# A planned AdaLN block on one core: smaller last pieces, split statistics and another list of leads

## The chip, the core and the metric

The kernel runs on one core of a Trainium2 chip, whose other cores do nothing. Five engines take part, each with an instruction queue of its own that runs in order: TensorE (PE in the profile; PEld is its weight load), VectorE (DVE), ScalarE (ACT), GpSimd (POOL) and SyncE (SP), which here only issues DMA transfers. The metric is the device time of one execution in microseconds (us), from several runs of which the median is taken.

## The reference

The input `x` holds 8 batches of 1024 tokens with 128 features, in float32. Six modulation vectors come from a conditioning vector `c`, and two sub-blocks are added onto `x`:

```python
mod = (_silu(L0_c) @ L0_wmod).reshape(B, 6, 1, -1)
sa, ca, ga, sb, cb, gb = (mod[:, 0], ..., mod[:, 5])
ga = (2 * (ga >= 0) - 1) * jnp.maximum(jnp.abs(ga), 0.25)      # gb likewise
h = _layernorm(x, axis=-1) * (1 + ca) + sa
x = x + ga * attn(h)
h = _layernorm(x, axis=-1) * (1 + cb) + sb
x = x + gb * ffn(h)
```

`attn` is six layers of linear attention, each followed by a multilayer perceptron:

```python
for i in range(6):
    xn = _layernorm(x, ln1_w[i], ln1_b[i])
    q, k, v = heads(xn @ wq[i]), heads(xn @ wk[i]), heads(xn @ wv[i])   # 8 heads of 16
    context = einsum('bhnd,bhne->bhde', softmax(k, over tokens), v)
    x = merge(einsum('bhnd,bhde->bhne', softmax(q, over features), context)) @ wo[i] + bo[i] + x
    hdn = leaky_relu(_layernorm(x, ln2_w[i], ln2_b[i]) @ w1[i], 0.01)   # 128 -> 512
    x = hdn @ w2[i] + x                                                 # 512 -> 128
```

`ffn` has 352 hidden features and rounds both operands of each product to a four-bit float grid, with one scale for every 16 values (`fp4_quant_dequant`):

```python
gate, y = fp4_linear(x, w_gate), fp4_linear(x, w_up)
return fp4_linear(silu(gate) * y, w_down)
```

## The kernel before

A batch lies in SBUF as 128 partitions by 8 chunks (`C`) of 128 features, token = partition x 8 + chunk. It is worked on in two halves (`H`) of 4 chunks (`HC`), 512 columns each, which is one PSUM bank. Four lanes (`LANES`) hold the buffers of four batches, so up to four batches are under way; batch b+4 takes the buffers of batch b.

Each batch passes eight stages: stage 0 is the first modulated layernorm, stages 1 to 6 are the six layers, stage 7 is the FFN and the store. `layernorm` (L571) makes per chunk one `bn_stats` (L587) and one `bn_aggr` (L589) on VectorE, then for the half a logarithm and an exponential on ScalarE (L603, L608), four small VectorE steps that refine the reciprocal root and make the shift (L613 to L629), and last the scaled rows, half on VectorE (L635) and half on ScalarE (L642). The eight statistics instructions of a half are one step, `moments`. `transposed` (L655) turns a half with TensorE (L661). A layer then has its products on TensorE (keys L892, queries L939, the context L1002 to L1036, the output L1069, the perceptron L1115 and L1132), its softmaxes on VectorE and ScalarE with the query scaling on POOL (L980), and its additions onto `x` on VectorE (L1054).

`ffn` (L1145) takes the modulated norm of both halves, rounds each half (`fp4`, L668), and turns it. For every chunk there are two products of 352 columns (L1176), the silu on ScalarE (L1184) and the gate's product on VectorE (L1192). The gated values lie in four groups (`NQ`) of G = 2 chunks, 704 columns. Each group is rounded by `fp4`: on VectorE a maximum per 16 values (L689), the scale (L696), its reciprocal (L701) and a product (L705); on ScalarE the magnitude (L715); on VectorE two steps that round (L719, L726); on POOL the product with the scale (L733). Then TensorE turns the group (L1207), ScalarE copies it out of PSUM (L1222), TensorE multiplies it by `w_down` with the modulation folded in (L1233) and VectorE adds it onto `x` (L1242). After the second and fourth group a half of 256 KB is stored (L1250). The buffers of `fp4` and the turned group `gT` exist twice, and groups alternate between the two sets.

Nothing is issued while this code runs. Every piece of work is a step handed to a planner (`Plan`), with its engine, its estimated time (`occ`), what it reads and writes, and a priority. `Plan.order` (L143) then simulates the engines and puts the steps in one order. At each turn it takes, over all engines, the step that can start first by its estimate; among those that start together, the one with the longest chain of work behind it (`tail`) plus its lead. The lead comes from the table `LEAD[batch][stage]`; `TURNS` changes entries of it at given times of the simulation, as (time, [(batch, stage, lead), ...]). Steps without a stage, such as the preparation of weights and of the later modulation (`aside`), have the lead -`LATE`, in part with more taken off. Steps with `port=True` on VectorE and all on POOL are kept apart by the simulation, so that the two do not use the port to SBUF that they share at one time. Eight PSUM banks are handed out by the simulation too.

The planner also keeps TensorE's clock up. Where TensorE would stand still for more than `GAP` (0.6 us), it puts in dummy products of the identity with itself (`warm`, L1287) into a free bank, and stops `BRINK` short of the next real step. Before the time `COLD` it takes a dummy product for twice as long. The resulting order is fixed by dependencies between neighbours on each engine's queue.

Of the kernel before, what the change touches and what calls it, by code (L numbers as in the profile page):

```python
# [14 lines left out]
P = 128  # L15
# [47 lines left out]
class Ps:  # L63


    n = 0
# [17 lines left out]
class Plan:  # L84
# [5 lines left out]
    GAP, BRINK, COLD = 0.6, 0.15, 6.0  # L90
# [52 lines left out]
    def order(self, leads, turns, warm):  # L143
# [17 lines left out]
        while todo:  # L161
# [22 lines left out]
            gap = e == "PE" and t - free[e] > self.GAP  # L184
            while gap and min(bank_free) <= free[e]:
                to = free[e] + (2 if free[e] < self.COLD else 1) * mm(P)
                if to > t - self.BRINK:
                    break
                w, bank = Step(), bank_free.index(min(bank_free))
                w.fn, w.func = lambda bank=bank: warm(bank), None  # L190
                free[e] = bank_free[bank] = to
                out.append(w)
# [3 lines left out]
            end = now + s.occ  # L196
# [38 lines left out]
def mm(n):  # L235

    return 0.01 + n * 1.66e-3
# [11 lines left out]
def kernel(  # L249
# [41 lines left out]
        [2428, 4186, 594, 344, -1166, -1149, -1333, -3656],  # L291
        [-878, 557, 2162, 224, -3438, -84, 492, -1524],
        [1136, -253, -1456, -2344, -3625, 1683, -2362, -2313],
# [8 lines left out]
        (75, [(1, 1, 582)]),  # L302
        (90, [(3, 1, 625)]),
        (135, [(2, 2, -1493)]),
        (315, [(2, 2, -332)]),
        (330, [(2, 2, -1493)]),
        (435, [(1, 4, -3891)]),
        (450, [(1, 4, -3438)]),
        (480, [(2, 4, -5886)]),
        (495, [(2, 4, -3663)]),  # L310
        (675, [(2, 7, -1993), (4, 2, -2394), (4, 3, -1963)]),
        (840, [(4, 4, -73)]),
        (1050, [(5, 6, -1896)]),
        (1095, [(4, 6, -2129)]),
        (1125, [(4, 6, -55), (5, 7, -1056)]),
        (1185, [(4, 7, -1051)]),
        (1215, [(6, 6, -416), (6, 7, -409)]),
        (1230, [(7, 5, -1069)]),
        (1245, [(4, 7, -1061)]),
        (1275, [(7, 5, -1070), (7, 6, -414)]),  # L320
        (1350, [(7, 6, -432)]),
        (1365, [(6, 7, -1605), (7, 7, -1614)]),
    ]
    LATE = 70.0
    NQ = 4
    FCOLS = C // NQ * I

# [243 lines left out]
    def layernorm(ln, dst, src, h, n, HV=HC // 2):  # L571


        stats = Buf(lanes_p, [P, HC, 6], f"stats{h}{ln}", f"stats_{n}{h}")
# [9 lines left out]

        def moments():
            for c in range(HC):
                nc.vector.bn_stats(stats.ap()[:, c, :], s(c))  # L587
# [3 lines left out]
        add("DVE", HC * 0.264, moments, r=at(src, h), w=[stats, mv])  # L591
# [76 lines left out]
    def fp4(src, parts, ncol, n, i):  # L668
# [13 lines left out]
        def each(t):  # L682
# [47 lines left out]
        )  # L730
        add(
            "POOL", pool2(ncol),
            lambda: nc.gpsimd.tensor_tensor(  # L733
                blocks(src()), blocks(vv()), each(s()), ALU.mult
            ),
            r=[v, scale], w=parts,
# [408 lines left out]
    def ffn(x, mod, b, ln):  # L1145
# [49 lines left out]
        for i, g in enumerate(gs):  # L1195
            fp4(lambda g=g: g.ap()[:, : G * I], g.parts, G * I, f"g{b}_{i}", i % 2)

            gT = Buf(work, [P, NK * G * P], f"gT{i % 2}", f"gT_{b}_{i}", 2)
            whole = I // P
            tts = [Ps(psum), Ps(psum)]  # L1200

            def turn(g, tt, m0, m1):
                for m in range(m0, m1):
                    k, kk = KS[m]
                    for c in range(G):
                        o = ((m - m0) * G + c) * P
                        nc.tensor.transpose(  # L1207
                            tt.ap()[:kk, o : o + P],
                            g.ap()[:, c * I + k : c * I + k + kk], ident,
                        )  # L1210

            for part, (m0, m1) in enumerate(((0, whole), (whole, NK))):
                kk = KS[m1 - 1][1]
                n = (m1 - m0) * G * P
                add(
                    "PE", (m1 - m0) * G * TRANSPOSE,
                    lambda g=g, tt=tts[part], m0=m0, m1=m1: turn(g, tt, m0, m1),
                    r=[g], w=[tts[part]],
                )
                add(  # L1220
                    "ACT", act(n),
                    lambda gT=gT, tt=tts[part], m0=m0, kk=kk, n=n: nc.scalar.copy(  # L1222
                        gT.ap()[:kk, m0 * G * P : m0 * G * P + n], tt.ap()[:kk, :n]
                    ),
                    r=[tts[part]], w=[gT[part]],
                )
            td = Ps(psum)

            def dmm(gT=gT, td=td):
                for c in range(G):  # L1230
                    for m, (k, kk) in enumerate(KS):
                        o = (m * G + c) * P
                        nc.tensor.matmul(  # L1233
                            td.ap()[:, c * D : (c + 1) * D], gT.ap()[:kk, o : o + P],
                            wdb.ap()[:kk, m, :], start=(m == 0), stop=(m == NK - 1),
                        )

            add("PE", G * NK * mm(D), dmm, r=[gT, wdb], w=[td])

            def onto(i=i, td=td):  # L1240
                xc = x.ap()[:, i * G * D : (i + 1) * G * D]
# [107 lines left out]
```

## Time and profile before

| what | before |
|---|---|
| median of 3 runs | 1419.99 us (1418.98 to 1420.02) |
| profiled execution: its time | 1418.91 us |
| profiled execution: its span, first to last instruction | 1417.3 us |
| granted clock of TensorE over the span | 0.999 |
| TensorE busy | 1400.6 us, of it 33.5 in tile `warm` |
| VectorE busy | 1148.7 us |
| ScalarE busy | 987.7 us |
| POOL busy | 249.7 us |
| last store issued, and landed after | 1414.1 us, 2.0 us |

A row of a group or of a timeline gives the engine, the line of the kernel, the operation, what it writes and reads by the program's tile names, the shapes and the count. In a timeline the two numbers in front are the start and the time covered in us; what stands in brackets is how long the engine stood idle before it and whose work ended that. A float32 product appears as two MATMUL records, a float32 turn as one. Matmuls overlap in their pipeline, so a record's duration (275 ns for 128 columns) is longer than the distance from one to the next (0.11 us). VectorE's records overlap a little in the same way.

### The profile page before, as it was taken

How to read it: one execution, taken by the hardware profiler on the slowest of the kernel's cores; microseconds unless marked ns; L12 is line 12 of the kernel's file. 1: busy time of each engine (PE TensorE's matmuls, PEld its weight loads, DVE VectorE, ACT ScalarE, POOL GpSimd, SP SyncE). 2: the span in 40 equal slices, each digit the busy share in tenths (PEclk: the TensorE clock that was granted, in tenths of full speed). 3: DMA queues.
4: the chain of work that ended last, by engine and by line, in shares of the span. 5: the costliest groups of instructions: out<-in, count | busy, mean ns of one | idle time of the engine just before them, and what ended most of it. 6: DMA issues, size and time to landing. Idle time of an engine off the chain costs nothing. (4 is left out here: it accounts for less than half of the span.)

```text
span 1417.3 us, 26401 instructions
## 1 busy us (share of the span) xinstructions
PE 1400.6 (99%) x9257; PEld 1124.6 (79%) x9257; DVE 1148.7 (81%) x4491; ACT 987.7 (70%) x2286; POOL 249.7 (18%) x215
## 2 busy tenths in 40 slices
PE   9999999999999999999999999999999999999998
PEld 7787788787787788778877887778778887787787
DVE  8996768776688887798989886587897767999986
ACT  6885856766667767676766675676776667867763
POOL 2220101010112112122231110011223111112222
PEclk9999999999999999999999999999999999999999
DMA  7100000000000000000000000000000000000000
GB/s 224 39 1 1 2 1 1 1 2 1 1 16 12 1 16 1 15 12 16 17 26 1 16 1 1 1 1 1 12 16 1 1 1 1 1 1 5 5 23 31
DMA packets 16004, 18.78 MB, mean 13 GB/s; under 512 B 1552, under 2 KB 9848, under 8 KB 15872
## 3 DMA queue, kind: packets, MB, share of 16 engines
q1 hardware_dynamic: 15872, 17.10, 3.8%
q8 instruction: 73, 1.20, 0.4%
q14 instruction: 59, 0.48, 0.1%
HBM read 12.88 MB, written 4.22 MB: 12 GB/s over the span
## 5 line engine op out<-in xcount | busy, mean ns | idle before, releaser
L1115 PE MATMUL ps<-xT_m,w_sb 128*128 128x512 f32 x768 | 349.7, 593 | 1.5 <-DVE g L1192 1.2
L1115 PEld LDWEIGHTS ps<-xT_m,w_sb 128*128 128x128 f32 x768 | 137.2, 190 | 132.0 <-issue 92.5
L980 POOL TENSOR_TENSOR q<-q,qsum 128x512 f32<-128x512 f32 x96 | 102.2, 1073 | 629.5 <-DVE qsum L975 195.2
L1054 DVE TENSOR_TENSOR x<-ps,x 128x512 f32<-128x512 f32 x192 | 129.9, 681 | 101.4 <-PE ps L1132 83.3
L603 ACT ACTIVATE rstd_a<-mv_a,eps 128x4 f32<-128x4 f32 x96 | 28.6, 298 | 125.3 <-DVE mv_a L589 105.2
L939 PEld LDWEIGHTS ps<-wq_sb,xT_a 128*128 128x128 f32 x768 | 95.5, 192 | 24.3 <-issue 16.3
L642 ACT ACTIVATE xh_a<-x,shift_a,rstd_a 128x128 f32<-128x128 f32 x192 | 84.0, 489 | 38.0 <-DVE shift_a L629 36.8
L1132 PEld LDWEIGHTS ps<-w_sb,hT_D 128*128 128x128 f32 x640 | 86.8, 192 | 15.0 <-issue 11.7
L939 PE MATMUL ps<-wq_sb,xT_a 128*128 128x128 f32 x768 | 98.2, 275 | 0.5 <-ACT g L1184 0.5
L1132 PE MATMUL ps<-w_sb,hT_E 128*128 128x128 f32 x640 | 97.6, 275 | 0.0
L1132 PE MATMUL ps<-w_sb,hT_C 128*128 128x128 f32 x640 | 97.6, 275 | 0.0
L1132 PE MATMUL ps<-w_sb,hT_B 128*128 128x128 f32 x640 | 97.6, 275 | 0.0
L1132 PE MATMUL ps<-w_sb,hT_D 128*128 128x128 f32 x640 | 97.5, 275 | 0.0
L1069 PEld LDWEIGHTS ps<-m,qT 128*128 128x128 f32 x768 | 91.1, 192 | 7.3 <-issue 2.8
L892 PE MATMUL ps<-xT_a,wk_sb 128*128 128x512 f32 x192 | 95.4, 595 | 1.0 <-ACT xT_a L872 0.6
L1069 PE MATMUL ps<-m,qT 128*128 128x128 f32 x768 | 95.2, 276 | 0.8 <-DVE m L1043 0.8
L1002 PEld LDWEIGHTS ps<-k,xh_a 128*128 128x128 f32 x768 | 90.5, 192 | 6.5 <-issue 3.8
L1002 PE MATMUL ps<-k,xh_a 128*128 128x128 f32 x768 | 93.4, 275 | 0.2 <-DVE x L1054 0.2
L642 ACT ACTIVATE xh_m<-x,shift_m,rstd_m 128x128 f32<-128x128 f32 x192 | 82.6, 489 | 10.5 <-DVE shift_m L629 9.9
L872 ACT ACTIVATE xT_a<-ps,cols 128x512 f32<-128x512 f32 x96 | 72.1, 775 | 19.2 <-PE ps L661 18.8
L587 DVE BATCH_NORM_STATS2 stats_a<-x 128x6 f32<-128x128 f32 x384 | 82.9, 278 | 2.9 <-POOL x L855 0.9
L1132 PEld LDWEIGHTS ps<-w_sb,hT_B 128*128 128x128 f32 x640 | 84.4, 192 | 0.5 <-ACT xh_m L642 0.2
(180 smaller groups left out, 3263.8 us busy)
## 6 DMA issues: line engine op xcount, KB each, us to landing
x<-in_L_attn_x_dram SPq DMA_DIRECT2D x16, 256.0 KB, 3.3
out_dram<-x SPq DMA_DIRECT2D x16, 256.0 KB, 2.0
w_sb<-in_L_attn_w_dram SPq DMA_DIRECT2D x12, 256.0 KB, 4.3
mod<-mod_d SPq DMA_DIRECT2D x8, 256.0 KB, 3.7
mod<-mod_d SPq DMA_DIRECT2D x4, 128.0 KB, 3.6
wmod_b<-in_L_wmod_dram SPq DMA_DIRECT2D x1, 384.0 KB, 3.6
wk_sb<-in_L_attn_wk_dram SPq DMA_DIRECT2D x6, 64.0 KB, 3.5
wq_sb<-in_L_attn_wq_dram SPq DMA_DIRECT2D x6, 64.0 KB, 3.5
```

The lines of the kernel that those rows point to most:

```text
L587: nc.vector.bn_stats(stats.ap()[:, c, :], s(c))
L603: lambda: nc.scalar.activation(y(), var(), AF.Ln, bias=eps),
L642: nc.scalar.activation(d(c), s(c), AF.Identity, bias=shift.ap()[:, c : c + 1], scale=rstd.ap()[:, c : c + 1],)
L872: lambda t=t, h=h: nc.scalar.activation(half(xT, h), t.ap(), AF.Identity, bias=col(params + 1, l), scale=col(params, l),),
L892: lambda tk=tk, h=h: nc.tensor.matmul(tk.ap(), wk_sb[:, l, :], half(xT, h), start=True, stop=True),
L939: nc.tensor.matmul(tq.ap()[:, c * D : (c + 1) * D], half(xT, h)[:, c * P : (c + 1) * P], wq_sb[:, l, :], start=True, stop=True,)
L980: lambda h=h, hs=hs: nc.gpsimd.tensor_tensor(heads(half(q, h)), heads(half(q, h)), each(qsum.ap()[:, hs]), ALU.mult),
L1002: nc.tensor.matmul(tc_.ap()[:, :D], chunks(xh.ap())[:, c, :], chunks(k.ap())[:, c, :], start=(c == 0), stop=(c == C - 1),)
L1054: lambda: nc.vector.tensor_tensor(half(x, h), t.ap(), half(x, h), ALU.add),
L1069: nc.tensor.matmul(to.ap()[:, c * D : (c + 1) * D], half(qT, h)[:, c * P : (c + 1) * P], m.ap(), start=True, stop=True,)
L1115: lambda th=th, h=h, j=j: nc.tensor.matmul(th.ap(), w1_sb[:, l, j * P : (j + 1) * P], half(xmT, h), start=True, stop=True,),
L1132: nc.tensor.matmul(ty.ap()[:, c * D : (c + 1) * D], hidden(j)[:, c * P : (c + 1) * P], w2g.ap()[:, j, :] if l == L - 1 else w2_sb[:, l, j, :],
```

## The change

Four things are changed together.

- The last batch's FFN ends in smaller pieces. The work behind the gates is moved into a function `down`, which is called for every entry of `PIECES`: for batches 0 to 6 four groups of two chunks, as before; for batch 7 two groups of two chunks and then four of one chunk. Of the last piece alone `fp4` does the final product with the scale on VectorE instead of POOL. Batch 7 is stored in four parts of 128 KB, each after its two chunks, instead of two of 256 KB. The pieces still alternate between two sets of buffers.
- The statistics of a half are no longer one step. Each of its four `bn_stats` is a step of its own, which depends on the part of the source that it reads, and the four `bn_aggr` are one more step. The planner may place other VectorE work between them.
- In the planner `COLD` is 7.5 instead of 6.0. Before that time a real TensorE step takes twice its estimate in the simulation, and a gap is filled with dummy products from half of `GAP` on.
- The leads are others: a few entries of `LEAD`, the whole list `TURNS` (57 times instead of 21), and `LATE` is 140 instead of 70.

What is computed stays the same.

```diff
-    GAP, BRINK, COLD = 0.6, 0.15, 6.0
+    GAP, BRINK, COLD = 0.6, 0.15, 7.5
...
-            gap = e == "PE" and t - free[e] > self.GAP
+            cold = 2 if e == "PE" and free[e] < self.COLD else 1
+            gap = e == "PE" and t - free[e] > self.GAP / cold
             while gap and min(bank_free) <= free[e]:
-                to = free[e] + (2 if free[e] < self.COLD else 1) * mm(P)
+                to = free[e] + cold * mm(P)
...
-            end = now + s.occ
+            end = now + s.occ * (2 if e == "PE" and now < self.COLD else 1)
...
     LEAD = [
-        [2428, 4186, 594, 344, -1166, -1149, -1333, -3656],
-        [-878, 557, 2162, 224, -3438, -84, 492, -1524],
-        [1136, -253, -1456, -2344, -3625, 1683, -2362, -2313],
+        [2420, 4178, 586, 336, -1174, -1157, -1341, -3664],
+        [158, 557, 2162, 224, -3448, -84, 492, -1524],
+        [1202, -253, -1456, -2344, -3625, 1683, -2362, -2313],
...
     TURNS = [
-        (75, [(1, 1, 582)]),
-        (90, [(3, 1, 625)]),
...
-        (1350, [(7, 6, -432)]),
-        (1365, [(6, 7, -1605), (7, 7, -1614)]),
+        (15, [(2, 1, -124)]),
+        (45, [(0, 2, 1600), (3, 0, -324)]),
...
+        (1305, [(6, 7, -440), (7, 6, -443)]),
+        (1320, [(7, 6, 40)]),
+        (1335, [(4, 7, -2064), (5, 7, -2271), (6, 7, -2282), (7, 6, 278), (7, 7, 207)]),
     ]
-    LATE = 70.0
+    LATE = 140.0
...
+    PIECES = (
+        [(i, i * C // NQ, C // NQ) for i in range(NQ)],
+        [(0, 0, 2), (1, 2, 2), (0, 4, 1), (1, 5, 1), (0, 6, 1), (1, 7, 1)],
+    )
+    DVE_LAST = True
...
+        for c in range(HC):
+            add(
+                "DVE", 0.197, lambda c=c: nc.vector.bn_stats(stats.ap()[:, c, :], s(c)),
+                r=at(src, h)[c * H // HC :][:1], w=[stats[c]],
+            )
+
         def moments():
             for c in range(HC):
-                nc.vector.bn_stats(stats.ap()[:, c, :], s(c))
-            for c in range(HC):
                 nc.vector.bn_aggr(mv.ap()[:, c, :], stats.ap()[:, c, :])

-        add("DVE", HC * 0.264, moments, r=at(src, h), w=[stats, mv])
+        add("DVE", HC * 0.067, moments, r=[stats], w=[mv])
...
-    def fp4(src, parts, ncol, n, i):
+    def fp4(src, parts, ncol, n, i, last="POOL"):
...
-        add(
-            "POOL", pool2(ncol),
-            lambda: nc.gpsimd.tensor_tensor(
-                blocks(src()), blocks(vv()), each(s()), ALU.mult
-            ),
-            r=[v, scale], w=parts,
+        eng = nc.vector if last == "DVE" else nc.gpsimd
+        add(
+            last, (vec if last == "DVE" else pool2)(ncol),
+            lambda: eng.tensor_tensor(blocks(src()), blocks(vv()), each(s()), ALU.mult),
+            r=[v, scale], w=parts, port=True,
         )
...
+        for i, c0, cn in PIECES[b == B - 1]:
+            down(gs[c0 // G], c0 % G, cn, c0, wdb, x, f"{b}_{c0}", i % 2, DVE_LAST and b == B - 1 and c0 + cn == C)
+            done = c0 + cn
+            if b == B - 1 and done % G == 0:
+                parts, n = [x[done // G - 1]], G
+            elif b < B - 1 and done % HC == 0:
+                parts, n = at(x, done // HC - 1), HC
+            else:
+                continue
+            add(
+                "SP", move(64 * n),
+                lambda done=done, n=n: nc.sync.dma_start(
+                    out[:, done - n : done, :], chunks(x.ap())[:, done - n : done, :]
+                ),
+                r=parts,
+            )
+
+    def down(g, g0, G, c0, wdb, x, name, i, last):
+        def src():
+            return g.ap()[:, g0 * I : (g0 + G) * I]
+
+        parts = g.parts[g0 : g0 + G]
+        fp4(src, parts, G * I, f"g{name}", i, "DVE" if last else "POOL")
+
+        gT = Buf(work, [P, NK * C // NQ * P], f"gT{i}", f"gT_{name}", 2)
...
+        add("PE", G * NK * mm(D), dmm, r=[gT, wdb], w=[td])
...
+        add("DVE", vec(G * D), onto, r=[td], w=[x[c0 // (C // NQ)]])
```

## The prediction

> **What bounds the kernel now.** First I read the page's busy times and its slices.
>
> ```profile
> PE 1400.6 (99%) x9257; PEld 1124.6 (79%) x9257; DVE 1148.7 (81%) x4491; ACT 987.7 (70%) x2286; POOL 249.7 (18%) x215
> ...
> PE   9999999999999999999999999999999999999998
> ...
> PEclk9999999999999999999999999999999999999999
> ```
>
> TensorE (PE) is busy for 99% at the full granted clock, so only the matmul time itself seems to be left. But part of that busy time is filler: the planner puts dummy matmuls (tile `warm`) into TensorE's gaps. So the second view is busy time by stretches, first of everything, then (after its own heading line) of tile `warm` alone.
>
> ```profile
> 0.00:100.00 100.00, 95.11 (x641) 77.77 (x642) 91.65 (x451) 75.71 (x200) 26.79 (x32) 1.00 0.31 94
> 100.00:600.00 500.00, 499.56 (x3324) 400.85 (x3323) 378.99 (x1563) 345.11 (x809) 61.34 (x56) 1.00 0.02 5
> 600.00:1372.00 772.00, 764.87 (x4997) 609.77 (x4997) 646.76 (x2411) 546.91 (x1238) 149.94 (x120) 1.00 0.02 7
> 1372.00:1418.00 46.00, 41.10 (x302) 36.15 (x300) 31.26 (x68) 20.02 (x43) 11.62 (x8) 0.97 0.08 30
> ...
> core 0: us, PE busy (x) PEld busy (x), PEclk, DMA share, GB/s
> 0.00:100.00 100.00, 17.35 (x124) 15.91 (x124) 1.00 0.31 94
> 100.00:600.00 500.00, 0.00 (x0) 0.00 (x0) 1.00 0.02 5
> 600.00:1372.00 772.00, 4.47 (x30) 3.81 (x30) 1.00 0.02 7
> 1372.00:1418.00 46.00, 11.70 (x96) 11.27 (x96) 0.97 0.08 30
> ```
>
> Columns: PE, PEld, DVE, ACT, POOL busy, clock, DMA. Idle plus filler on TensorE is the loss: 4.9 + 17.4 = 22.2 us in the first 100; 0.4 in the next 500; 7.1 + 4.5 = 11.6 from 600 to 1372; and 4.9 (4.2 without the 0.7 behind the span) + 11.7 = 15.9 at the end. Together 50 us. The change removes no matmul, so it can work on these 50 us alone.
>
> Last, the timeline of the end.
>
> ```profile
> 1396.32 2.39 PE L1289 MATMUL warm<-ident 128*128 128x128 f32 x20
> ...
> 1403.71 5.08 PE L1289 MATMUL warm<-ident 128*128 128x128 f32 x44
> ...
> 1405.73 1.69 DVE L726 SCALAR_TENSOR_TENSOR fv_g<-fmag_g,fv_g 128x704 f32<-128x704 bf16 x2
> 1406.70 3.31 POOL L733 TENSOR_TENSOR g<-fv_g,scale_g 128x704 f32<-128x704 f32 x2 [6.43 <-DVE fv_g L726]
> ...
> 1410.07 0.87 PE L1207 MATMUL ps<-ident,g 128*128 128x128 f32 x6
> 1410.78 2.84 PE L1233 MATMUL ps<-wdb,gT 128*128 128x128 f32 x24
> ...
> 1413.66 0.42 DVE L1242 TENSOR_TENSOR x<-ps,x 128x256 f32<-128x256 f32 x1 [0.92 <-PE ps L1233]
> ```
>
> VectorE (DVE) is gapless from 1388.2 to 1407.4: there it is the bound, and TensorE only warms. Then two quantized groups of two chunks wait one behind the other for POOL (3.31 us), and 1.4 + 2.8 us of turning and matmuls follow.
>
> **The change part by part.**
>
> *Pieces at the end.* VectorE's rows in that stretch start 0.80 apart at 704 columns and 0.43 apart at 352 (the gate, L1192). Four large steps per group, two groups made into four pieces: 8 x (2 x 0.43 - 0.80) = +0.5 us. The small scale step and the reciprocal (0.09 and 0.34 apart; I take 0.2 for half the reciprocal) add 2 x 0.09 + 2 x 0.06 = +0.3. Two adds (0.33 apart at 256 columns, so about 0.2 at 128) that used to follow the last quantization become three that lie ahead of its end: +0.6. The last scaling moves from POOL to VectorE: +0.43. VectorE thus ends 1.8 us later, at about 1409.2, but with everything done. Behind it: turns 0.5 (three at 0.11 and a drain of 0.16), the second copy 0.35 (379 ns for 256 columns), three matmuls 0.85, the add 0.35 with its latency: 2.1, so 1411.3 where 1414.1 stood: **-2.8**.
>
> Against it stands a wait that the diff adds without naming it: the buffers scale, rec, fv, fmag and gT alternate between two sets, so the third piece's reduction (L689) waits until POOL has scaled the first, and the fourth's until the second. VectorE queues behind that reduction all its later steps. POOL's one row at 352 columns is 788 ns; the gates that cover this wait before (POOL's 3.25 us at 1397.0 beside 1.81 us of L1192) lie earlier now. Bounds: 0, if the adds and the other piece fill it, to 2 x 0.79 = 1.6; I take the middle, +0.8, since two pieces in flight offer some 3.8 us of vector work against a latency of about 3.6 for one.
>
> The Trainium skill speaks against the split: "VectorE: DVE Perf Modes", § Rules for kernel authors, asks for the fewest operations. By that rule alone the split would only cost, 0.8 us by the rows above for its 12 more instructions; by the same rows the end behind VectorE falls from 6.7 to 2.1.
>
> *Last store.* 128 KB instead of 256 KB; four in place of two on SP, which has nothing else then. Issue to landing is 2.0 us for 256 KB stores; of the loads, 256 KB take 3.7 and 128 KB 3.6. Bounds 0 to -1; I take **-0.1**. "DMA: Bandwidth & Descriptors", § Anatomy of one DMA, gives a fixed 2 us plus bytes at 436 GB/s, which would make it -0.3, but also 2.6 us for a store that lands in 2.0 here.
>
> *Filler before the end.* New turns raise batch 7's last stages at 1320 and 1335 and push the other FFNs behind. Warm rows of 2.2 us at 1379.0 and 0.8 at 1390.7 stand where TensorE ran out of other batches' FFN work while batch 7's own chain was late. Bounds -3 to +3 (all of it filled; as much again); I take **-1**.
>
> *Statistics as single steps.* The same 4 x 0.21 and one 0.36 us, so no cost by itself (VectorE idles 19% of the span, and no wait is added across engines). The gain is where a small step waited for a block: at 17.3 to 20.0 the four dependent steps L613 to L629 of batch 0 each stand behind a 1.06 us block of statistics of batch 1.
>
> ```profile
> 17.32 0.12 DVE L613 SCALAR_TENSOR_TENSOR shift_a<-mv_a,rstd_a 128x4 f32<-128x4 f32 x1
> 17.37 0.85 DVE L587 BATCH_NORM_STATS2 stats_i<-x 128x6 f32<-128x128 f32 x4
> ```
>
> Between single steps that chain needs 4 x 0.2 and a few 0.21s, some 1.6 us less until the first turn (21.04). How much reaches the end is another matter, since VectorE is full from 15 to 54 whatever its order.
>
> *LATE, COLD, the new order at the start.* LATE 140 holds back preparation; VectorE spends 3.5 us on it before 60 (L557 1.35, the mod8 steps 2.2). COLD changes what the planner believes: the 512-column matmuls at 7.4 to 9.3 still take 1042 ns, the next ones 427 for 256 columns, so the clock rises at about 9 us of the trace. "TensorE: Matmul & The Clock Gate", Part 1, says not to fit to a cold count, as the window runs free. At worst warm matmuls sit before a real one, 0.45 us each. With the statistics: bounds -5 (3.5 + 1.6) to +2 (four such); I take **-1.5**, nearer to nothing because the vector sum is unchanged.
>
> *The middle.* The order from 100 to 1372 is new everywhere. Its 12.0 us are some ten gaps of 0.2 to 2.7 us, mostly on VectorE (xh_m 1.3, g 2.1, ctxT 0.7 and the 2 us of filler ahead of it). The stretch to 600 shows that an order with 0.4 us in 500 exists at 76% of VectorE; after 600 it is at 84%, and the FFNs fall there. Bounds -12 to +12 (none, or twice as many); finer steps can answer the VectorE waits, so I take a quarter: **-3**.
>
> **Sum.** -2.8 + 0.8 - 0.1 - 1 - 1.5 - 3 = -7.6, against the profiled execution's 1418.9 us (span 1417.3): 1411.3. The median of the runs is 1.1 above that execution, so 1412.4; I say 1412.
>
> **The rivals.**
> *Only the end gains.* The middle and the start come out even (as many new gaps as closed): -2.1 to -3: 1417 to 1418. For it: the old order also looked full. Against: the blocks seen to hold small steps are gone.
> *Nearly all closes.* -2 at the end, -3 filler, -10 middle, -3 start: 1402. Against: an FFN needs about 30 us of VectorE (four groups at 3.6, two halves at 2.8, gates 3.4, adds 1.3, norms and wdb some 5) for 19 of TensorE (32 records at 0.30, 88 at 0.11), so gaps late in the run are not only a matter of order.
> *Slower: FFNs pile up.* That surplus of 11 us is hidden by layers, where TensorE leads (148 records at 0.11 and 20 at 0.43, 25 us, against (1149 - 8 x 30) / 48 = 19 of VectorE). If the late turns for batches 4 to 6 leave one more whole FFN uncovered behind 1335, TensorE waits 11 us more; less the 4.6 from end and start, 1425, and 1426 by the median. It decides from about 5 us, half an FFN, on. For it: VectorE is at 43.3 of 45 us from 1300 to 1345. Against: batch 7's layer, which needs covering most, goes first.
> *The split doesn't pay.* The buffer wait of 1.6 and POOL holding VectorE (L635 took 1.66 instead of 0.58 for two beside POOL at 1354.6) eat the end's gain: 1414, inside my range.
>
> **How the numbers follow.** The forecast (1406 to 1417) 0.50, with the failed split inside it; only the end 0.18 (1416 to 1420); nearly all closes 0.12 (1400 to 1406); piling up 0.20 (1421 to 1429). A measurement of this kernel can tell 0.2%, 2.8 us. Faster than 1417.2: 0.50 + 0.12 + a third of 0.18 = 0.68. Slower than 1422.8: four fifths of 0.20, 0.16. Between: 0.16. The range 1401 to 1423 leaves out a sixth of the fast case and three quarters of the slow one, 0.17 in all; the likeliest case's own is 1406 to 1417.
>
> **What would show it.** Right: tile `warm` under 33.5 us, its part after 1372 (or the last 45 us) down from 11.7 to below 9; one-chunk L705 to L726 rows and no POOL row behind the last; from the last quantizing row to the last add 2 to 3 us instead of 6.7; L613 to L629 of batch 0 without a 1.06 us step between. Wrong: POOL-ended waits of L689 over 1 us in the last 12 us, filler or DVE-ended TensorE waits of more than 12 us between 100 and 1372, or a first turn later than 21.

## The result, and the profile after

The changed kernel takes 1405.74 us (median of 4 runs, 1405.16 to 1407.13); the kernel before took 1419.49 us beside it (4 runs, 1417.75 to 1420.02). The ratio is 0.9907, with a 95% interval of 0.989 to 0.9924: 13.8 us faster by the medians, 0.9% by the ratio. The profiled execution of the changed kernel took 1406.12 us, with a span of 1404.4 us, against 1418.91 and 1417.3.

The page's busy times and slices of the changed kernel look like those of before: TensorE is at 99% again.

```profile
PE 1391.3 (99%) x9181; PEld 1116.3 (79%) x9181; DVE 1142.5 (81%) x4506; ACT 983.0 (70%) x2292; POOL 247.7 (18%) x216
...
DVE  8998668487798687899667899988876748879897
...
PEclk9999999999999999999999999999999999999999
```

The gain is seen only by stretches. These are the windows of the changed kernel, first of everything, then of tile `warm` alone (the columns are the same as in the prediction).

```profile
0.00:100.00 100.00, 94.97 (x651) 78.45 (x652) 93.03 (x452) 73.36 (x198) 26.08 (x32) 1.00 0.31 94
100.00:600.00 500.00, 498.80 (x3268) 396.96 (x3268) 386.07 (x1579) 345.13 (x814) 69.73 (x61) 1.00 0.02 7
600.00:1359.00 759.00, 756.50 (x4967) 605.04 (x4966) 625.90 (x2386) 542.89 (x1231) 137.93 (x113) 1.00 0.02 6
1359.00:1405.00 46.00, 41.03 (x300) 35.87 (x298) 37.50 (x91) 21.59 (x50) 13.99 (x11) 0.99 0.10 36
...
0.00:100.00 100.00, 15.23 (x112) 14.17 (x112) 1.00 0.31 94
100.00:600.00 500.00, 0.00 (x0) 0.00 (x0) 1.00 0.02 7
600.00:1359.00 759.00, 0.61 (x4) 0.53 (x4) 1.00 0.02 6
1359.00:1405.00 46.00, 7.78 (x58) 7.11 (x58) 0.99 0.10 36
```

As in the prediction, a stretch's loss is its length (up to the end of the span) less TensorE's busy time, plus `warm`. The last stretch is always the last 46 us, and what is left of the span without the losses is called matmul time.

| kernel | 0 to 100 | 100 to 600 | 600 to the last 46 | last 46 | loss | matmul time |
|---|---|---|---|---|---|---|
| before | 22.2 | 0.4 | 11.6 | 15.9 | 50.2 | 1367.1 |
| changed | 20.3 | 1.2 | 3.1 | 12.2 | 36.7 | 1367.7 |
| difference | -2.0 | +0.8 | -8.5 | -3.7 | -13.5 | +0.6 |

So 7.7 of the 13.5 us lie between 100 us and the last 46 us, where most of the gaps and the filler are gone, and about a quarter lies at the end. The last rows of the timeline show the end: one-chunk rows on VectorE, no POOL row behind the last rounding (L773), and 2.9 us from the end of that rounding (1398.87) to the end of the last add (1401.77), where 6.7 stood before.

```profile
1398.35 0.52 DVE L773 SCALAR_TENSOR_TENSOR fv_g<-fmag_g,fv_g 128x352 f32<-128x352 bf16 x1
...
1398.91 0.53 DVE L781 TENSOR_TENSOR g<-fv_g,scale_g 128x352 f32<-128x352 f32 x1
...
1400.51 0.94 PE L1302 MATMUL ps<-wdb,gT 128*128 128x128 f32 x6
1401.48 0.29 DVE L1311 TENSOR_TENSOR x<-ps,x 128x128 f32<-128x128 f32 x1 [1.40 <-PE ps L1302]
```

### The profile page after: what moved, and what is told of

Its sections match the earlier page's. It is cut to its first block, busy times and chain, and to the rows that moved or that the text cites. A ratio compares the mean times of both kernels' runs of the same rounds, so it can differ in the third digit from the quotient of the medians.

```text
span 1404.4 us, 26348 instructions
## 1 busy us (share of the span) xinstructions
PE 1391.3 (99%) x9181; PEld 1116.3 (79%) x9181; DVE 1142.5 (81%) x4506; ACT 983.0 (70%) x2292; POOL 247.7 (18%) x216
## 4 chain that ended last, share of the span: by engine, by line
PE 88%; DVE 7%; ACT 2%; SPq 1%; DMA 1%; issue 1%; POOL 0%; POOLq 0%; ACTq 0%; DVEq 0%
PE ps L1178 22%; PE ps L1161 22%; PE ps L708 11%; PE ps L1048 6%; PE ps L938 5%; PE ps L1115 5%; PE ps L985 5%; PE ps L1222 5%; PE ps L1302 3%; PE ps L1278 1%; SPq L417 1%; DVE x L1100 1%; PE ps L1082 1%; PE ps L1057 1%; DMA x<-in_L_attn_x_dram 1%; DVE stats_m L630 1%
## 5 line engine op out<-in xcount | busy, mean ns | idle before, releaser
L1161 PE MATMUL ps<-xT_m,w_sb 128*128 128x512 f32 x768 | 352.0, 595 | 0.3 <-ACT xT_m L918 0.3
L1161 PEld LDWEIGHTS ps<-xT_m,w_sb 128*128 128x128 f32 x768 | 137.6, 191 | 128.8 <-issue 95.6
L918 ACT ACTIVATE xT_m<-ps,cols 128x512 f32<-128x512 f32 x96 | 72.1, 776 | 20.1 <-PE ps L708 20.0
```

Source lines behind the costliest of these rows:

```text
L918: lambda t=t, h=h: nc.scalar.activation(half(xT, h), t.ap(), AF.Identity, bias=col(params + 1, l), scale=col(params, l),),
L1161: lambda th=th, h=h, j=j: nc.tensor.matmul(th.ap(), w1_sb[:, l, j * P : (j + 1) * P], half(xmT, h), start=True, stop=True,),
```

## The experiments

The theory at the outset: the middle gains because small urgent VectorE steps are no longer held behind a block of eight statistics, and the end gains by the one-chunk pieces. The rivals: the gain is that of the new leads alone; the end gains by its order and not by its pieces; the dummy products, of which there are fewer, hold the clock up or cost the time. In the course of the runs a further cause appeared that neither kernel's planner sees: GpSimd steps that start ahead of their planned place.

**The statistics.** Both kernels keep the changed kernel's planned order and gather, after planning, the five statistics steps of each half into one block: once at the place of the first of them, once at the place of the last.

```diff
-    for step in plan.order(LEAD, TURNS, warm):
+    for step in gathered(plan.order(LEAD, TURNS, warm)):
```

> The changed kernel with its own order, in which only the four statistics instructions and the aggregation of a half are put back together into one block, at the place of the first. Theory A (single steps close the gaps in the middle, because small urgent vector steps no longer stand behind a 1.06 us block): 165 of 224 halves have other work between their statistics, so the time goes back by most of the middle's gain, 4 to 8 us, to 1410 to 1414, and TensorE's loss between 600 and the last 46 us rises from 3.1 us to over 7. Theory B (the order found by the search closes them, the split only lets the planner see finer): within 1.5 us of the changed kernel, loss in the middle under 5 us.

Measured: 1417.73 us (11 runs, 1416.31 to 1421.38), ratio to before 0.9999 (0.999 to 1.0008). All of the gain is gone, more than theory A expected. The losses become 22.6, 2.2, 6.5 and 12.2 us, 6.8 more than in the changed kernel, none of it at the end; the matmul time rises by 4.8 us to 1372.5. One place shows idle time and a slow clock together. Here is VectorE's timeline of this kernel, then TensorE's, then TensorE's windows (busy, clock, DMA):

```profile
667.29 1.27 DVE L947 TENSOR_REDUCE nmax<-ps 128x1 f32<-128x512 f32 x2
668.49 0.86 DVE L630 BATCH_NORM_STATS2 stats_a<-x 128x6 f32<-128x128 f32 x4
669.26 0.36 DVE L637 BATCH_NORM_AGGREGATE mv_a<-stats_a 128x2 f32<-128x6 f32 x4
669.54 0.12 DVE L954 TENSOR_TENSOR nmax<-nmax 128x1 f32<-128x1 f32 x1
...
670.53 0.66 PE L710 MATMUL ps<-ident,kT 128*128 128x128 f32 x4 [1.89 <-ACT kT L963]
...
668.00:670.00 2.00, 0.64 (x6) 1.00 0.03 8
670.00:672.00 2.00, 1.47 (x10) 0.78 0.01 4
672.00:674.00 2.00, 2.00 (x6) 0.50 0.00 0
674.00:676.00 2.00, 2.00 (x16) 0.87 0.00 0
```

The 0.12 us step that ends the maximum of the keys (L954) stands behind 1.05 us of statistics of another half; ScalarE's exponential (`kT`) waits for it, TensorE for that, 1.89 us, and then the granted clock falls to 0.50. In the changed kernel one single statistic lies between the same steps:

```profile
659.76 1.28 DVE L945 TENSOR_REDUCE nmax<-ps 128x1 f32<-128x512 f32 x2
660.96 0.28 DVE L630 BATCH_NORM_STATS2 stats_a<-x 128x6 f32<-128x128 f32 x1
661.16 0.14 DVE L952 TENSOR_TENSOR nmax<-nmax 128x1 f32<-128x1 f32 x1
```

The control puts the block at the place of the last step:

> Control to the first run: the changed kernel with its own order, the four statistics and the aggregation of a half again as one block, but at the place of the aggregation, so that urgent steps go ahead of the statistics and only the statistics' own chain can be late. If the 11.6 us of the first run came from urgent steps behind the block (theory A): at most 4 us slower than the changed kernel, no nmax step behind a block near 661 us, no clock below 0.9 there. If any shift in a tuned order costs as much (rival): 8 to 14 us again.

Measured: 1418.3 us (11 runs, 1416.8 to 1419.48), ratio 0.9996 (0.9987 to 1.0004); losses 22.1, 1.0, 7.4 and 12.6, matmul time 1372.7. A block costs as much here as there. So it is shown that this order needs the single steps, worth 12.0 and 12.6 us to it. That they pay by letting urgent steps through is not shown, not even at the place above. In the control the same step (L954) follows its maximum directly, and TensorE waits for `kT` all the same, 1.77 us (the clock stays at 1.00 behind this wait):

```profile
668.00 0.16 DVE L954 TENSOR_TENSOR nmax<-nmax 128x1 f32<-128x1 f32 x1
...
669.02 0.66 PE L710 MATMUL ps<-ident,kT 128*128 128x128 f32 x4 [1.77 <-ACT kT L963]
```

The two maxima (L945 in the changed kernel) begin 0.1 us after the queries' products begin in the changed kernel, 1.0 us after in the kernel above and 1.8 in the control. So with blocks VectorE's work as a whole comes late against TensorE's here, and the wait is not that of one step behind one block alone. A block at the last place delays the half's own chain, and that costs the same. The theory in its narrow form is not confirmed; by which path the blocks cost their 12 us stays open.

**The leads.** `LEAD`, `TURNS` and `LATE` of before, in the otherwise changed kernel.

```diff
-    LATE = 140.0
+    LATE = 70.0
...
     LEAD = [
-        [2420, 4178, 586, 336, -1174, -1157, -1341, -3664],
+        [2428, 4186, 594, 344, -1166, -1149, -1333, -3656],
...
```

> The changed kernel with the leads, turns and LATE of before. Theory (the gain in the middle is the searched order, and a list of leads fits only the steps that it was searched for): slower than before, 1440 to 1480 us, nearly all of it as filler and idle on TensorE between 100 us and the end. Rival (the smaller steps bring the gain, any sensible leads do): 1412 or faster.

Measured: 1459.87 us (4 runs, 1458.99 to 1461.27), ratio 1.0288 (1.0273 to 1.0303). The losses are 28.2, 2.0, 36.1 and 21.1 us. A list of leads that served one list of steps loses 54 us on another that differs little, so this kernel doesn't tell what the new leads would be worth without the new steps. `LATE` was undone only together with them and `COLD` not at all, so neither has a price of its own. One entry of the list is easier to price:

```diff
-        (1335, [(4, 7, -2064), (5, 7, -2271), (6, 7, -2282), (7, 6, 278), (7, 7, 207)]),
```

> The changed kernel without the last entry of its turns (at 1335, which puts batch 7's last layer and FFN ahead of the FFNs of batches 4 to 6). The order is the same up to there. Theory (this entry keeps other batches' FFN work back as filler for batch 7's own chain; the prediction took 1 us of it, 3 at most): 3 to 6 us slower, all of it in the last 60 us. Rival (the end is set by VectorE's sum): within 1 us.

Measured: 1410.94 us (4 runs, 1409.86 to 1411.95), ratio 0.9942 (0.9927 to 0.9957), 5.2 us more than the changed kernel. The earlier stretches stay (20.9, 1.2, 3.7); the last one loses 18.0 instead of 12.2, nearly all of it filler where TensorE ran out of other batches' FFN work. Tile `warm` in the last 46 us of this kernel, against 7.78 above:

```profile
1364.00:1410.00 46.00, 13.90 (x104) 12.79 (x104) 0.98 0.09 32
```

**The pieces.** All batches end in two-chunk groups that are scaled on POOL, under the new leads.

```diff
-        [(0, 0, 2), (1, 2, 2), (0, 4, 1), (1, 5, 1), (0, 6, 1), (1, 7, 1)],
+        [(i, i * C // NQ, C // NQ) for i in range(NQ)],
...
-    DVE_LAST = True
+    DVE_LAST = False
```

> The changed kernel with batch 7's FFN in four two-chunk groups, all scaled on POOL, leads as they are (the order differs from about 1270 of the planner's time on). The prediction gave the pieces 2.8 less 0.8 us: theory, 2 to 5 us slower, in the last 46 us alone, and 6 to 7 us from the last rounding step to the last add. Rival (VectorE's 12 more instructions eat it): within 1 us.

Measured: 1412.12 us (4 runs, 1410.52 to 1413.09), ratio 0.9949 (0.9935 to 0.9964), 6.4 us more, where 2 to 5 were expected. The end looks like that of before again, with two groups behind one another on POOL:

```profile
1400.02 1.69 DVE L773 SCALAR_TENSOR_TENSOR fv_g<-fmag_g,fv_g 128x704 f32<-128x704 bf16 x2
1400.99 3.31 POOL L781 TENSOR_TENSOR g<-fv_g,scale_g 128x704 f32<-128x704 f32 x2 [6.41 <-DVE fv_g L773]
...
1407.95 0.42 DVE L1311 TENSOR_TENSOR x<-ps,x 128x256 f32<-128x256 f32 x1 [0.92 <-PE ps L1302]
```

From the last rounding's end to the last add's it takes 1408.37 - 1401.71 = 6.7 us again. The last 46 us lose 16.9 instead of 12.2 (+4.7); the remaining 2.0 us lie before, in an order that was made for other pieces.

Three smaller parts of the end were undone alone, in the same order. The last scaling on POOL:

```diff
-            lambda: eng.tensor_tensor(blocks(src()), blocks(vv()), each(s()), ALU.mult),
+            lambda: nc.gpsimd.tensor_tensor(blocks(src()), blocks(vv()), each(s()), ALU.mult),
```

> The changed kernel in the same order, only the very last scaling on POOL instead of VectorE. POOL's one-chunk rows are 0.78 to 1.0 us, VectorE's is 0.53: theory, 0.3 to 0.6 us slower, the last add later by that. Rival: the last piece waits for something else (the third piece's matmuls on TensorE), then no difference above 0.1 us.

Measured: 1405.68 us (4 runs, 1404.34 to 1407.32), ratio 0.991 (0.9897 to 0.9924): no difference that the times can tell. In the trace POOL takes 0.79 us where VectorE took 0.53, and from the last rounding's start to the last add's it takes 3.37 instead of 3.13 us. One last store of 256 KB instead of two of 128 KB:

> The changed kernel with one last store of 256 KB instead of two of 128 KB. The prediction took 0.1 us for the half size; the traces have 3.2 us from the last issue to the end of the span before and 2.6 after. Theory (the end of the span follows the size): 0.4 to 0.6 us slower, 3.1 us from issue to end. Rival (the fixed part of a store rules): under 0.2 us.

Measured: 1405.24 us (4 runs, 1404.63 to 1407.55), ratio 0.9911 (0.9895 to 0.9926). From the issue of the last store to the end of the span it takes 3.0 us instead of 2.6; the times don't tell it. The third was to give the last two pieces buffers of their own:

```diff
-        [(0, 0, 2), (1, 2, 2), (0, 4, 1), (1, 5, 1), (0, 6, 1), (1, 7, 1)],
+        [(0, 0, 2), (1, 2, 2), (0, 4, 1), (1, 5, 1), (2, 6, 1), (3, 7, 1)],
```

> The changed kernel in the same order, the third and fourth one-chunk pieces with buffers of their own. The prediction put +0.8 us (0 to 1.6) on the wait of their reductions for POOL: if it costs that, 0.8 us faster. If the order hides it (the trace shows one such wait of 0.17 us), within 0.3 us.

Measured: 1404.34 us (4 runs, 1404.2 to 1406.55), ratio 0.9904 (0.9891 to 0.9918). This experiment failed in its making: `ffn` hands `i % 2` on, so pieces 2 and 3 use the sets 0 and 1 as before, and the kernel is the changed one over again. It says nothing of the wait; it repeats the result, and shows that two medians of one kernel can lie 1.4 us apart. What the wait costs is read from the trace of the changed kernel alone: the third piece's reduction (L736) stands 0.17 us behind POOL, the fourth's not at all.

```profile
1392.82 0.52 DVE L736 TENSOR_REDUCE scale_g<-g 128x22 f32<-128x352 f32 x1 [0.17 <-POOL g L781]
...
1394.93 0.51 DVE L736 TENSOR_REDUCE scale_g<-g 128x22 f32<-128x352 f32 x1
```

**The filler.** The dummy products planned for after 60 us are left out.

```diff
-                out.append(w)
+                if to < 60.0:
+                    out.append(w)
```

> The changed kernel without the dummy matmuls after 60 us of the planner's time; the order of all else is the same. Theory (the filler keeps the clock up): records of 128 columns after the gaps of the last 20 us take about 0.5 us instead of 0.275, granted clock below 1 there, 1 to 3 us slower. Rival (no gap there is long enough): same clock, within 0.5 us.

Measured: 1405.91 us (4 runs, 1404.74 to 1407.32), ratio 0.991 (0.9894 to 0.9927). In the profiled execution the clock stays at 1.00 to the last turn, with gaps at the end of up to 1.1 us in which nothing runs. But this was the one of four executions with a mean clock of 1.000. The other three, of which there is no profile, had 0.997 and 0.998, and the changed kernel's four 0.999 and 1.000. So the late filler makes no difference that the medians show, and `warm` after 60 us is a measure of TensorE's waits rather than their price; that it does nothing for the clock is not shown. The dummy products of the first 60 us were never left out.

**One gap in the middle.** The longest gap that the changed kernel has left in the middle is followed by a slow clock in its profiled execution. Its timeline, then TensorE's windows:

```profile
791.36 1.32 POOL L1130 TENSOR_TENSOR w2g<-w_sb,mod 128x512 f32<-128x512 f32 x1 [12.37 <-DVE shift_m L665]
791.36 1.34 DVE L670 SCALAR_TENSOR_TENSOR rstd_m<-shift_m,rstd_m 128x4 f32<-128x4 f32 x2
792.62 1.29 POOL L901 TENSOR_TENSOR h<-h,mod 128x512 f32<-128x512 f32 x1
...
792.70 1.30 DVE L676 SCALAR_TENSOR_TENSOR shift_m<-mv_m,rstd_m 128x4 f32<-128x4 f32 x2
...
794.31 1.68 PE L708 MATMUL ps<-ident,xh_m 128*128 128x128 f32 x8 [1.25 <-DVE xh_m L682]
...
796.32 8.83 PE L1161 MATMUL ps<-xT_m,w_sb 128*128 128x512 f32 x16 [0.34 <-ACT xT_m L918]
...
796.00:798.00 2.00, 1.68 (x2) 0.63 0.00 0
798.00:800.00 2.00, 2.00 (x4) 0.51 0.00 0
```

TensorE waits 1.25 us for normalized rows, because two pairs of VectorE steps of 128x4 take 1.34 and 1.30 us instead of the 0.23 that the pair before them took. Each of them runs beside a POOL step. From 796 to 800 the clock is at 0.63 and 0.51. The first attempt was to fill the gap with six dummy products ahead of the turn (step 5024 of the order):

```diff
+FILL = 5024, 6
...
+            if n == FILL[0]:
+                for _ in range(FILL[1]):
...
+                    w.fn, w.func = lambda bank=bank: warm(bank), None
+                    out.append(w)
```

> The changed kernel in the same order with six dummy matmuls (1.3 us) in one place, the gap at 793.1 us that the planner did not foresee (1.25 us idle, then 512-column records at a granted clock of 0.63 and 0.51 for some 4 us). Theory (such a gap lets the clock fall, and its price is the 1.7 us of slow matmuls as much as the idle time): clock 1.00 in that stretch and 1.5 to 1.9 us faster. Rival (the clock falls for another reason, or the filler delays the turn): within 0.5 us.

Measured: 1405.58 us (4 runs, 1404.82 to 1405.82), ratio 0.9903 (0.9889 to 0.9916). The clock stays at 1.00, but the time does not fall: the dummies, 12 records one after another in one bank, last until 796.19, though the first row for the turn starts on VectorE at 794.09, 0.17 us later than in the changed kernel, whose turn began at 794.31, and the real turn starts at 796.25. What the clock gave, the filler took.

Nor does this run show that the filler held the clock. Behind the same gap, with nothing put into it, the clock also stays at 1.00 in the profiles of three kernels above: the one without the last entry of `TURNS`, the one without late filler, and the one with one last store, of which these are TensorE's rows:

```profile
794.51 1.68 PE L708 MATMUL ps<-ident,xh_m 128*128 128x128 f32 x8 [1.32 <-DVE xh_m L682]
796.53 7.13 PE L1161 MATMUL ps<-xT_m,w_sb 128*128 128x512 f32 x16 [0.34 <-ACT xT_m L918]
```

The second attempt removes the cause of the gap. The planner's simulation keeps POOL's steps and the `port=True` steps of VectorE apart; on the chip nothing does. Every POOL step now also waits for the last VectorE step with `port=True` that stands ahead of it in the planned order; order and work are unchanged.

```diff
+    held = mybir.DependencyInfo(mybir.DependencyClass.Sync, mybir.DependencyReason.DATA)
...
         for i in new:
+            if getattr(step, "eng", None) == "POOL" and port_last:
+                tc.add_manual_dep(i, port_last, held, reason="port")
...
+            if getattr(step, "eng", None) == "DVE" and step.port:
+                port_last = i.name
```

> The changed kernel in the same order, with every POOL step also waiting for the last VectorE step ahead of it in the order that shares its port (the order assumes this, the program so far does not ask for it). At 791.4 POOL starts on w2g 1.5 us ahead of its place in the order, and two pairs of small VectorE steps take 1.3 us each instead of 0.2. Theory (POOL holding the port makes that gap): the pairs take 0.2 to 0.3, the gap of 1.25 us and the fall of the clock go, 2.5 to 3.5 us faster. Rival (the vector steps are late for another reason, or the added waits cost elsewhere what they bring): within 1 us.

Measured: 1399.08 us (4 runs, 1398.9 to 1400.03), ratio to before 0.986 (0.9845 to 0.9875): 6.7 us faster than the changed kernel, where 2.5 to 3.5 were expected. Beside the two executions of the changed kernel with a mean clock of 1.000 (1405.16 and 1405.37) it is 6.1 to 6.3 us. The same place in this kernel:

```profile
787.53 0.23 DVE L670 SCALAR_TENSOR_TENSOR rstd_m<-shift_m,rstd_m 128x4 f32<-128x4 f32 x2
...
787.75 0.23 DVE L676 SCALAR_TENSOR_TENSOR shift_m<-mv_m,rstd_m 128x4 f32<-128x4 f32 x2
...
789.07 1.04 PE L708 MATMUL ps<-ident,xh_m 128*128 128x128 f32 x8
789.15 1.30 POOL L1130 TENSOR_TENSOR w2g<-w_sb,mod 128x512 f32<-128x512 f32 x1 [14.00 <-DVE xh_m L682]
```

POOL starts behind the normalized rows, the pairs take 0.23 us each, and the turn has no gap before it. VectorE is busy 11 us less in all (1131.2) and POOL 10 us less (237.9): each had been holding the other. The losses are 19.5, 0.0, 1.7 and 13.5 us, 2.0 less than in the changed kernel, and the matmul time falls by 4.9 to 1362.7. Of that, 1.7 us are the sixteen records of L1161 behind the gap, which take 8.83 us in the changed kernel at the low clock and 7.13 here. The turn above shows another part: its eight records cover 1.68 us in the changed kernel, since they follow rows that come late, and 1.04 here. Such waits inside a group count as busy. The rest was not followed.

The added wait acts one way only. A VectorE step that stands behind a POOL step in the order can still start beside it: in batch 7's FFN one scale step of 22 columns (L743) takes 0.72 us instead of 0.11 in both kernels, each time beside a POOL step.

The same edit in the kernel before:

> The kernel before with the same single edit as the version of 1399.08 us: every GpSimd step also waits for the last VectorE step with port=True that stands ahead of it in the planned order. Order and contents unchanged. Theory: GpSimd steps that start ahead of their planned place and hold VectorE's small steps are a fault of both kernels, not of the new order; the kernel before has 11.6 us of idle and filler on TensorE from 600 us to 1372 us, and its pairs of small L618 to L629 steps beside GpSimd are stretched too. I expect 3 to 8 us less than before (1412 to 1417 us), a ratio to before of 0.994 to 0.998, with idle plus filler from 600 us on down by at least 3 us. Rival: the kernel before's gaps come from its order (statistics as blocks), not from GpSimd: within 1.5 us of before, or slower, because some GpSimd step that profited from its early start is late now.

Measured: 1409.35 us (5 runs, 1408.39 to 1409.74), ratio 0.9937 (0.9923 to 0.9951): 9.0 us less than before, more than expected. The losses are 21.0, 0.2, 7.1 and 16.5, of which the last two together are 3.9 less than before, and the matmul time is 1362.2, 4.9 less. The place of which the prediction had noted that L635 took 1.66 us instead of 0.58, in the kernel before and then with the edit:

```profile
1354.57 1.66 DVE L635 TENSOR_SCALAR xh_m<-x,mv_m,rstd_m 128x128 f32<-128x128 f32 x2
1354.65 1.49 POOL L733 TENSOR_TENSOR g<-fv_g,scale_g 128x704 f32<-128x704 f32 x1 [8.18 <-DVE shift_m L629]
...
1356.29 0.55 PE L661 MATMUL ps<-ident,xh_m 128*128 128x128 f32 x3 [0.64 <-DVE xh_m L635]
```

```profile
1344.66 0.59 DVE L635 TENSOR_SCALAR xh_m<-x,mv_m,rstd_m 128x128 f32<-128x128 f32 x2
...
1345.46 0.60 PE L661 MATMUL ps<-ident,xh_m 128*128 128x128 f32 x4
...
1346.52 1.39 POOL L733 TENSOR_TENSOR g<-fv_g,scale_g 128x704 f32<-128x704 f32 x1 [9.96 <-DVE x L1092]
```

With the wait on both sides the change is worth 0.986 / 0.9937 = 0.9923 by the ratios to before, in place of 0.9907. So the change and the wait are nearly independent; the difference, some 2 us, is no larger than the intervals. The gain in the middle stays as well: from 100 us to the last 46 the loss is 7.3 us in the kernel before with the wait and 1.7 in the changed one with it.

## Why the prediction was right, and where its sizes were off

1412 was forecast, with 1401 to 1423 as the range; 1405.74 was measured. The sum of 1411.3 stands against a profiled execution of 1406.1, and 4.7 of the 5.2 us between them are one term, the middle. The direction and the places were right. The measured median lies 0.3 us below the likeliest case's own interval, 1406 to 1417, in that of the rival in which nearly everything closes. By its own steps:

*Pieces, -2.8, with the buffer wait, +0.8.* VectorE was to end 1.8 us later, 0.43 of it the scaling, plus 0.8 for the wait: 2.2 to the end of the last rounding. From the end of the last gate and up products to there it took 13.4 us instead of 10.9, 2.5 more. Behind it were to stand 0.43 + 2.1 = 2.5 us; it was 2.9. So each part came within 0.4 us, both on the bad side: 2.5 - 3.8 = -1.3 instead of -2.0. But the 0.8 for the wait was right by luck. In the 13.4 us VectorE is idle for 1.0, in the 10.9 of before for 0.04. Only 0.17 us of this idle time ends with POOL, as was reckoned; 0.16 and 0.42 end with ScalarE's magnitude of the same piece (L762), a wait that the sum left out:

```profile
1397.79 0.53 DVE L766 SCALAR_TENSOR_TENSOR fv_g<-fmag_g,fv_g 128x352 f32<-128x352 bf16 x1 [0.42 <-ACT fmag_g L762]
```

The vector work itself grew by 1.55 us, near the 1.4 counted, but with rows in it that are longer beside POOL (L743 0.72 instead of 0.11, L752 0.80 instead of 0.51). The two stretches don't hold quite the same steps, so this division is rough, and the run that was to price the wait didn't. The rival in which the split doesn't pay falls: two-chunk groups lose 6.4 us in this order, 4.7 of it at the end. The rule of the Trainium skill that was weighed there, fewest operations ("VectorE: DVE Perf Modes", § Rules for kernel authors), asks for the slower version here: what decided was what stands behind VectorE's last instruction, 6.7 us against 2.9.

*Last store, -0.1.* From its issue to the span's end it took 2.6 us instead of 3.2 before, and 3.0 in the kernel with one last store. That is -0.4 to -0.6, inside the bounds of 0 to -1. The page "DMA: Bandwidth & Descriptors", § Anatomy of one DMA, gave -0.3, by a fit for DMAs that GpSimd issues, while SP issues these; a measured difference of 0.4 is nearer to it than the value that was taken, though the times don't tell either.

*Filler before the end, -1.* The measure was wrong, though the sum wasn't. Without the late filler the median is the same (1405.91), so this filler was no cost in itself that the times show. Its cause, waits for batch 7's chain, is what the entry at 1335 works on, and that one line of the table is worth 5.2 us. Yet without it the changed kernel's last 46 us lose 18.0, more than the 15.9 of before, so part of these 5.2 us mends what the rest of the new order would have done. The end as a whole was given -3.1 (pieces, wait, store, filler) and measured at -3.7: -1.3 and -0.6 by the lines above, and -1.8 left for this one, as a remainder.

*Statistics, LATE and COLD at the start, -1.5.* Measured -2.0. The first turn comes at 20.83 instead of 21.04, not 1.6 us earlier. The mechanism was right as far as the rows: single steps stand between L660 and L676 as foretold (before, two blocks stood between them, not one ahead of each), and the first normalized rows start on VectorE at 17.90 instead of 19.95. But TensorE runs dummy products that the planner put ahead of the turn until 20.8, when the four rows of the first half have been done since 18.96 (those of the second half are done at 20.56):

```profile
11.67 9.32 PE L1350 MATMUL warm<-ident 128*128 128x128 f32 x82
...
17.90 0.60 DVE L682 TENSOR_SCALAR xh_a<-x,mv_a,rstd_a 128x128 f32<-128x128 f32 x2
...
18.08 0.88 ACT L689 ACTIVATE xh_a<-x,shift_a,rstd_a 128x128 f32<-128x128 f32 x2
...
20.83 1.04 PE L708 MATMUL ps<-ident,xh_a 128*128 128x128 f32 x8
```

What the turn would gain without these dummies was not tried.

*The middle, -3.* This is the term that was mis-sized: from 100 us to the last 46 us the loss went from 12.0 to 4.3, -7.7. It was bounded by -12 and +12 and a quarter of the gain was taken, "finer steps can answer the VectorE waits". Nothing in the trace of before said how many they could answer. With blocks in the same order 12.0 to 12.6 us come back, so the finer steps carry the gain in this order; with the leads of before they lose 54 us, so they carry it only together with a list made for them. By which path they do was not shown. What an order made for blocks would give by as long a search was not tried and stays open.

*The rivals.* That only the end gains is out (-7.7 in the middle). Nearly everything closes, 1402, is nearer to 1405.74 than the forecast is: its -10 for the middle, -5 for the end with the filler and -3 for the start stand beside -7.7, -3.7 and -2.0. FFNs did not pile up: from 600 us to the last 46 TensorE idles for 2.5 us with 0.61 of filler. What would have shown the prediction wrong did not appear: the reduction's wait is 0.17 us, not over 1, and the first turn not later than 21.

*What it overlooked.* The row of 1.66 us for L635 beside POOL was used only as a price within one rival. It was a sample of something that cost the kernel before 9 us, more than any term of the sum, as taken or as measured.

## What to carry to other kernels

A planned order is only as good as what the chip does between its steps: an engine that the plan keeps off a shared port must be made to wait for it, because an early start, which costs nothing by the dependencies, can hold a small urgent step on another engine. A list of priorities that was made for one list of steps did not carry over to another one here; judge the two together, and undo a part in the fixed order to price it. And at the end of a kernel cut the last work so that little stands behind the last instruction of the engine that is full.

## What the runs showed of the hardware

*The clock can fall after short gaps, and the gap's length alone doesn't decide it.* In the changed kernel 1.25 us without matmuls, with 0.34 more behind the next turn, were followed by a granted clock of 0.63 and 0.51 until about 800. Seven kernels have this place in the same order and nothing put into it, with gaps of 1.24 to 1.32 us. In the profiles of four of them the clock falls to about half; in the other three it stays at 1.00, and the sixteen records of L1161 take 7.13 us instead of 8.83, so that a fall costs 1.7 us beside its gap. Elsewhere it is the same: behind a gap of 1.89 us the clock fell to 0.50 in the kernel with blocks, and behind another of 1.89 us, at 984.0, it stayed at 1.00 in the kernel with the old leads. Gaps of up to 1.1 us, one after another, left it at 1.00 at the end of the profiled execution without late filler, and so did one of 1.18 us in the kernel before. Of four executions of the changed kernel two had a mean clock of 1.000 (spans 1403.4 and 1403.7) and two of 0.999 (1404.4 and 1405.4). The Trainium skill ("TensorE: Matmul & The Clock Gate", Part 1) puts the fall after an idle window of about 3.4 us; the gaps between matmuls that a fall followed in these runs are 1.24 to 2.43 us long, and the measurement decides. Without a product, with turns only, the changed kernel has 3.3 us there (793.06 to 796.32); but 3.8 us of turns alone in the kernel before (787.37 to 791.15) left the clock at 1.00. What decides it stays open.

*POOL holds some of VectorE's steps for its whole instruction.* 128x4 pairs grew from 0.23 to 1.34 us, rows of 128x128 from 0.59 to 1.66 for two, each beside a POOL step of 1.3 to 1.5 us. Not every step is held: five statistics keep their 0.21 us each (1.03 in all) beside a POOL step of 1.27 us at 14.67 of the changed kernel. "SBUF — State Buffer", § Who interferes with whom, calls the pair of ports that the two engines share an exclusive lock, which goes to whoever issues first; these rows agree. That it is worth 6.7 to 9.0 us of a kernel in which POOL is busy for 18% had not been expected.
